# A graph attention kernel: queues of the opening stage, a staging pool of its own, and 17 of 18 edge tiles in two parts

## The chip, the cores and the metric

The kernel runs as one program on one core of a Trainium2 chip. The metric is the device time of one execution in microseconds (us). Engines are called TensorE (PE, with its weight loads shown as PEld), VectorE (DVE), ScalarE (ACT), GpSimd (POOL) and SyncE (SP), as in the profile. A queue is called by the engine that issues its transfers.

## The reference

Two graph attention layers stand between a normalization and residual paths. There are 3125 nodes with 768 features and 53125 edges, self loops among them, sorted by destination. All data is float32.

```python
def gat_conv(x, edge_index, W, a_src, a_dst, bias, heads, out_ch, concat):
    xl = (x @ W).reshape(n, heads, out_ch)
    alpha_src = jnp.einsum('nhc,hc->nh', xl, a_src)
    alpha_dst = jnp.einsum('nhc,hc->nh', xl, a_dst)
    e = jax.nn.leaky_relu(alpha_src[src] + alpha_dst[dst], 0.2)
    m = jax.ops.segment_max(e, dst, num_segments=n)
    e = jnp.exp(e - m[dst])
    s = jax.ops.segment_sum(e, dst, num_segments=n)
    alpha = e / (s[dst] + 1e-16)
    out = jax.ops.segment_sum(xl[src] * alpha[:, :, None], dst, num_segments=n)
    ...
h0 = jnp.maximum(_layernorm(x), 0.0)
h = gat_conv(h0, edge_index, W1, a_src1, a_dst1, b1, 4, 256, True)
h1 = relu(layer_norm(h, g1, be1)) + (h0 @ Wr1 + br1)
h = gat_conv(h1, edge_index, W2, a_src2, a_dst2, b2, 1, 768, False)
x + layer_norm(h, g2, be2) + (h1 @ Wr2 + br2)
```

Layer 1 has four heads of 256 channels, so W1 and Wr1 are 768 x 1024; W2 and Wr2 are 1024 x 768.

## The kernel before

**Tiling.** The nodes lie in NB = 25 blocks of P = 125. Edges of one block fill J = 18 tiles of 128 edges. Feature dimensions are cut into chunks of 128: NK1 = 6 for 768 and NK2 = 8 for 1024. Four blocks make a group of GB = 4, for which the residual product h0 @ Wr1 is made at once.

**The opening stage (0 to 209 us).** One loop, `for b in range(-2, NB + LAG)`, holds several streams. `fetch` loads a tile of x into one of eight buffers; tiles up to 4 are loaded by SP, later ones by POOL. `stats` (L600 to L604) and `normal` (L611, L612) make the layer norm on VectorE, with the square root `bn_sd` on ScalarE. `flip` transposes a block on TensorE (L623) and ScalarE writes it to `h0` (L625). `fill` is the generator `products` (L637 to L654): it multiplies a block by W1 (L645), ScalarE copies the two halves of 512 columns into `row` (L648, two buffers), and `store_rows` sends the finished row block to `table1` with two transfers on SP (L651). `work` is the generator `beside`: it counts edges by block (`edge_list`, L220, with a matmul over the counts at L228), has SP load the 25 edge windows of two kinds (`windows`, 50 loads), and folds the attention vectors into W1 on VectorE (`fold`, L308 and L309), which `alphas` (L633) needs. W1 is loaded by six transfers on ScalarE's queue (L691). The order of the instructions on ScalarE, VectorE and TensorE is the one written in the program, and an engine that waits holds what stands behind it.

**Softmax of layer 1 (209 to 481 us).** VectorE and TensorE compute the attention weights of all edges (L375 to L480); what remains of `products` is filled in on TensorE, and its last rows are drained after that.

**Between softmax and layer 1 (481 to 548 us).** VectorE folds the attention vectors of layer 2 into W2 (L730, L731), chunk by chunk, with tiles from a pool "wf". TensorE makes the residual product of group 0 (L739, 8 pieces of six matmuls, each recorded twice), ScalarE copies a piece to `rt0` (`copy_residual`, L577), and SP stores pairs of pieces into `r1T_d` (L581). The pool "rf" of `rt0` is opened after "wf" has been closed, so both lie on the same memory.

**Layer 1 (548 to 1547 us).** `sums` runs over the blocks. For each edge tile POOL gathers 128 rows of `table1` (L525, ten buffers), and VectorE makes a matrix `oh` (L536) that says which node of the block each edge ends at. A tile for which `split(j)` is true is multiplied by its attention weights in two parts: ScalarE makes a rounded product `hi` (four L543, one for each head) and VectorE the remainder in the place of `g` (four L544), and TensorE takes four matmuls of 512 columns in a faster float format (L548). A tile that isn't split has the weights multiplied into `oh` by ScalarE (four L558), and TensorE takes plain float32 matmuls of 256 columns, one for each head (L560). In between run the residual products of groups 1 to 6 (`residual`, L769) until about the 20th block, and behind each block its end, `end1`: layer norm, transposes (L801), relu (L803), residual added (L805), the product with W2 (L814). A block's last edge matmul is the one with the bias, L564.

```python
sums(H, C1, table1, al1, alo1_d, b1_r, lambda j: j % 9 != 4, 10, 4, 0, gp, pp, end1, later())
```

With `j % 9 != 4`, tiles 4 and 13 of 18 aren't split.

**Layer 2 (1547 to 2471 us)** repeats softmax and sums with one head of 768 channels.

Of the kernel before, what the change touches and what calls it, by code (L numbers as in the profile page):

```python
# [58 lines left out]
def in_order(  # L59
# [16 lines left out]
    nc = tc.nc  # L76
# [59 lines left out]
    def load_rows(q, t, src_, b):  # L136


        if b < NB - 1:
            q.dma_start(t, src_[b * P:b * P + 128, :])  # L140
        else:
            q.dma_start(t[:112], src_[b * P:b * P + 112, :])
            q.dma_start(t[112:P], src_[b * P + 112:(b + 1) * P, :])

    def store_rows(q, dst_, b, t):
        q.dma_start(dst_[b * P:b * P + 112, :], t[:112])
        q.dma_start(dst_[b * P + 112:(b + 1) * P, :], t[112:P])
# [424 lines left out]
    with tc.tile_pool(name="m1", bufs=1) as mp:  # L572
# [10 lines left out]
        with tc.tile_pool(name="w1", bufs=1) as wp, tc.tile_pool(name="pm1", bufs=1, space=PSUM) as pm1:  # L583
# [3 lines left out]
            with tc.tile_pool(name="d1", bufs=2) as dp, tc.tile_pool(name="pd1", bufs=1, space=PSUM) as pp:  # L587
                xts = {}

                def fetch(b):  # L590
                    xts[b] = dp.tile([128, D], F32, name="xt", bufs=AHEAD)
                    load_rows(nc.sync if b < 5 else nc.gpsimd, xts[b], x, b)

                found = {}

                def stats(b):
                    xt = xts[b][:P]
                    st = dp.tile([P, 2, 6], F32, name="bn_st", bufs=4)
                    for i in range(2):
                        nc.vector.bn_stats(st[:, i, :], xt[:, i * (D // 2):(i + 1) * (D // 2)])  # L600
                    mv = dp.tile([P, 2], F32, name="bn_mv", bufs=4)
                    nc.vector.bn_aggr(mv, st)
                    sd = dp.tile([P, 1], F32, name="bn_sd", bufs=4)
                    nc.scalar.activation(sd, mv[:, 1:2], AF.Sqrt, bias=eps[:P])  # L604
                    found[b] = mv, sd

                def normal(b):
                    xt = xts[b][:P]
                    mv, sd = found.pop(b)
                    rstd = dp.tile([P, 1], F32, name="bn_rs", bufs=4)  # L610
                    nc.vector.reciprocal(rstd, sd)  # L611
                    nc.vector.tensor_scalar(xt, xt, mv[:, 0:1], rstd, op0=OP.subtract, op1=OP.mult)  # L612

                def flip(b):

                    gi, o = b // GB, (b % GB) * P
                    if o == 0:
                        h0.append(wp.tile([128, NK1, min(GB, NB - b) * P], F32, name=f"h0_{gi}"))
                    xt = xts.pop(b)[:P]
                    for k0 in range(0, NK1, 3):  # L620
                        pt = pp.tile([128, 4, 128], F32, name="pt", bufs=3)
                        for k in range(3):
                            nc.tensor.transpose(pt[:, k, :P], xt[:, (k0 + k) * 128:(k0 + k + 1) * 128],  # L623
                                                ident[:P, :P])
                        nc.scalar.activation(h0[gi][:, k0:k0 + 3, o:o + P], pt[:, :3, :P], AF.Relu)  # L625
                    if b + AHEAD < NB:
                        fetch(b + AHEAD)

                def alphas(b):
                    gi, o = b // GB, (b % GB) * P  # L630
                    pa = pp.tile([P, 2 * H], F32, name="pas", bufs=1)
                    for k in range(NK1):
                        nc.tensor.matmul(pa, h0[gi][:, k, o:o + P], wa1[:, k, :],  # L633
                                         start=(k == 0), stop=(k == NK1 - 1))
                    return lambda: nc.vector.tensor_copy(asad1[:, b, :], pa)

                def products():  # L637

                    for b in range(NB):
                        gi, o = b // GB, (b % GB) * P  # L640
                        row = wp.tile([P, HC], F32, name="row", bufs=2)
                        for i in range(2):
                            pm = pm1.tile([128, 512], F32, name="pm", bufs=3)
                            for k in range(NK1):
                                nc.tensor.matmul(pm[:P], h0[gi][:, k, o:o + P], w1[:, k, i * 512:(i + 1) * 512],  # L645
                                                 start=(k == 0), stop=(k == NK1 - 1))
                                if k == NK1 - 1:
                                    nc.scalar.activation(row[:, i * 512:(i + 1) * 512], pm[:P], AF.Copy)  # L648
                                if k % 3 == 2:
                                    if i == 1 and k == NK1 - 1:  # L650
                                        store_rows(nc.sync, table1, b, row)  # L651
                                        if gi and (b % GB == GB - 1 or b == NB - 1):
                                            nc.sync.dma_start(h0T_d[gi][:, :, :o + P], h0[gi])
                                    yield  # L654

                fill = products()
                AHEAD, LAG = 8, 10

                def beside():

                    with tc.tile_pool(name="el", bufs=1) as ep:
                        listed = edge_list(ep, pp)
                        next(listed)
                        yield
                        for _ in listed:
                            yield
                    lists = windows(pp)
                    next(lists)
                    yield from fold(abs1, w1, NK1, H, C1, wa1)
                    for _ in lists:  # L670
                        yield

                work = beside()
                order = ctx.enter_context(ExitStack())
                order.enter_context(tc.manual_schedule(engines={PE}))
                with tc.manual_schedule(engines={ACT, DVE}):
                    fetch(0)
                    fetch(1)
                    next(work)
                    for b in range(2, 4):  # L680
                        fetch(b)
                    abs1 = folded(mp, H, C1, a_src1, a_dst1, "wr1", 2)
                    for b in range(4, AHEAD):
                        fetch(b)
                    late = None
                    for b in range(-2, NB + LAG):
                        if b + 2 < NB:
                            stats(b + 2)
                        if b == -1:
                            for k in range(NK1):  # L690
                                nc.scalar.dma_start(w1[:, k, :], W1[k * 128:(k + 1) * 128, :])  # L691
                        if 0 <= b + 1 < NB:
                            normal(b + 1)
                        if 0 <= b < NB:
                            flip(b)
                        if b >= 0:
                            next(work, None)
                        if late is not None:
                            late()
                            late = None  # L700
                        for _ in range(0 if b < 2 else 2 if b < LAG else 1 if b < NB or b % 2 else 0):
                            next(fill)
                        if b >= LAG:
                            late = alphas(b - LAG)
                    late()
                    for _ in work:
                        pass
                    for _ in range(3):
                        next(fill)
            with tc.tile_pool(name="pq1", bufs=1, space=PSUM) as pp:  # L710
# [6 lines left out]
                split_biases(mp)  # L717
                for _ in fill:
                    pass

                with tc.tile_pool(name="wf", bufs=2) as fp:
                    ab2 = fp.tile([128, 2, C2], F32, name="ab2", bufs=1)
# [7 lines left out]
                            nc.vector.tensor_tensor(t, w2k, ab2[:, i, :], OP.mult)  # L730
                            nc.vector.tensor_reduce(wa2[:, k, i:i + 1], t, axis=AX.X, op=OP.add)  # L731

                rp = order.enter_context(tc.tile_pool(name="rf", bufs=1))
                for m in range(NK2):
                    if m % 2 == 0:
                        rt = rp.tile([128, GB, 2, P], F32, name="rt0", bufs=4)
                    pm = pm1.tile([128, 512], F32, name="pm", bufs=3)
                    for k in range(NK1):
                        nc.tensor.matmul(pm[:, :GB * P], wr1[:, k, m * 128:(m + 1) * 128], h0[0][:, k, :],  # L739
                                         start=(k == 0), stop=(k == NK1 - 1))  # L740
                    copy_residual(0, rt, pm, m, GB)
# [3 lines left out]
        with tc.tile_pool(name="w2", bufs=1, reuse_waits="tile") as wp, tc.tile_pool(name="e1", bufs=2, reuse_waits="tile") as ep, \  # L745
# [74 lines left out]
                        nc.vector.tensor_copy(asad2[:, b, :], pm[:, 384:n])  # L820
                store_rows(nc.sync, table2, b, row)

            sums(H, C1, table1, al1, alo1_d, b1_r, lambda j: j % 9 != 4, 10, 4, 0, gp, pp, end1, later())


    with tc.tile_pool(name="m2", bufs=1, reuse_waits="tile") as mp, \
# [556 lines left out]
```

## Time and profile before

| what | value |
|---|---|
| time, median of three runs | 2466.43 us |
| time, lowest and highest of the three | 2462.73 and 2474.13 us |
| the profiled execution's own time | 2472.55 us |
| its span (first to last instruction) | 2470.7 us |
| granted TensorE clock, mean of the span | 0.952 |
| busy PE / DVE / ACT / POOL | 2255.8 / 1941.0 / 1276.1 / 1138.2 us |
| bytes moved by DMA | 637.97 MB, mean 258 GB/s |
| opening stage, to the loop's end | 0 to 209 us |
| softmax of layer 1 and drained rows | 209 to 481 us |
| group 0's residual beside the fold of W2 | 481 to 548 us |
| layer 1 | 548 to 1547 us |
| layer 2 | 1547 to 2470.7 us |

The profiled execution is 6.1 us above the median of the three. A line of a group in the profile gives code line, engine, operation, the tiles (out<-in), the shapes and the count, then the busy time in us and the mean ns of one. A line of the waits gives the engine and code line that waited, the work that released it, and the sum, the number and the longest of the waits in us. A line of the windows gives a stretch, its length, and for each engine the busy time and the number of instructions, then the granted clock of TensorE, the busy share of the DMA engines and the GB/s moved. A busy TensorE isn't TensorE at its peak, and a matmul of plain float32 is recorded as two.

### The profile page before, as it was taken

What the parts mean: (1) busy time and instruction counts of PE and PEld (TensorE: products, weight loads), DVE (VectorE), ACT (ScalarE), POOL (GpSimd) and SP (SyncE); (2) the same over time, 40 slices, a digit from 0 to 9 for tenths busy, and PEclk for the clock granted to TensorE, in tenths of its full rate; (3) what the DMA queues carried; (4) which work ended last, traced back from release to release, by engine and by line L of the source; (5) the groups of instructions that cost most, each with busy time, mean ns of one, the idle gap of its engine ahead of it and who ended that gap; (6) DMA issues with size and microseconds to landing.
All of it is one profiled execution on the core that took longest, in us unless ns stands there. A gap on an engine that the chain in (4) does not pass through costs nothing.

```text
span 2470.7 us, 35867 instructions
## 1 busy us (share of the span) xinstructions
PE 2255.8 (91%) x11254; PEld 1477.1 (60%) x11254; DVE 1941.0 (79%) x4328; ACT 1276.1 (52%) x2687; POOL 1138.2 (46%) x980
## 2 busy tenths in 40 slices
PE   3898999959899999999999999799798998989987
PEld 2465665425566666666666776566476665656655
DVE  5845999647788888888889999587677776768777
ACT  1221332117788888888888898001244444444443
POOL 0000000006756565555555675000477777777775
PEclk9898999978999999999999999899899899999999
DMA  5453552429788888888988898784698898888886
GB/s 169 134 178 115 192 182 70 146 86 397 260 301 311 297 317 296 298 315 289 324 285 304 317 340 277 286 297 158 203 309 304 301 311 295 291 290 295 290 287 210
DMA packets 185508, 637.97 MB, mean 258 GB/s; under 512 B 31924, under 2 KB 49189, under 8 KB 184542
## 3 DMA queue, kind: packets, MB, share of 16 engines
q0 software_dynamic: 104032, 420.88, 49.9%
q1 hardware_dynamic: 76564, 201.94, 23.6%
q10 hardware_dynamic: 4714, 12.75, 1.5%
q8 instruction: 94, 1.54, 0.2%
q14 instruction: 104, 0.85, 0.1%
HBM read 567.40 MB, written 68.08 MB: 257 GB/s over the span
## 4 chain that ended last, share of the span: by engine, by line
PE 69%; DVE 17%; DMA 6%; issue 5%; SPq 1%; ACT 1%; POOL 0%; ACTq 0%; DVEq 0%; POOLq 0%
PE pa L548 22%; PE p L814 10%; PE pa L560 9%; PE pr L769 8%; PE pr L848 8%; PE pm L645 5%; DVE g L544 2%; DVE scr L394 2%; DVE al L397 2%; PE pq L392 1%; PE pas L633 1%; PE pm L739 1%; PE pa L564 1%; DMA g<-table,idx_s 1%; DMA bs<-slo_d 1%
## 5 line engine op out<-in xcount | busy, mean ns | idle before, releaser
L525 POOL DMA_INDIRECT g<-table,idx_s x900 | 1064.4, 1183 | 958.7 <-DMA ab<-in_L_gnn_a_dst_dram 349.4
L543 ACT ACTIVATE hi<-g,al 128x256 fp32r<-128x256 f32 (+1 forms) x1925 | 966.6, 578 | 495.2 <-DMA g<-table,idx_s 177.8
L544 DVE SCALAR_TENSOR_TENSOR g<-g,al,hi 128x256 fp32r<-128x256 f32 (+1 forms) x1925 | 993.2, 566 | 78.7 <-issue 44.5
L548 PE MATMUL pa<-hi,oh 128*125 128x512 f32 (+1 forms) x1450 | 585.9, 482 | 41.6 <-issue 27.3
L548 PE MATMUL pa<-g,oh 128*125 128x512 f32 (+1 forms) x1450 | 448.4, 385 | 35.7 <-issue 30.5
L548 PEld LDWEIGHTS pa<-hi,oh 128*125 128x125 f32 x1450 | 268.1, 189 | 228.8 <-issue 119.0
L548 PEld LDWEIGHTS pa<-g,oh 128*125 128x125 f32 x1450 | 268.1, 189 | 97.1 <-issue 45.0
L848 PE MATMUL pr<-wr,h 128*125 128x384 f32 x800 | 308.6, 518 | 4.1 <-issue 2.7
L536 DVE TENSOR_SCALAR oh<-iota_f,rel_s 128x128 fp32r<-128x128 f32 x775 | 211.5, 283 | 127.2 <-PE pa L548 92.8
L560 PE MATMUL pa<-g,w 128*125 128x384 f32 (+1 forms) x900 | 291.7, 455 | 10.0 <-issue 8.4
L814 PE MATMUL p<-w,h1T 128*125 128x384 f32 (+1 forms) x800 | 298.5, 492 | 1.5 <-DVE h1T L805 1.5
L645 PE MATMUL pm<-w,h 128*125 128x512 f32 x600 | 285.2, 625 | 0.0
L769 PE MATMUL pr<-h0k,wr 128*128 128x500 f32 (+1 forms) x576 | 260.5, 538 | 1.9 <-DMA h0k<-h0T_d 1.9
L560 PEld LDWEIGHTS pa<-g,w 128*125 128x125 f32 x900 | 170.9, 194 | 96.9 <-issue 46.0
L848 PEld LDWEIGHTS pr<-wr,h 128*125 128x125 f32 x800 | 155.0, 199 | 92.1 <-issue 23.5
L814 PEld LDWEIGHTS p<-w,h1T 128*125 128x125 f32 x800 | 148.0, 188 | 78.5 <-issue 10.1
L645 PEld LDWEIGHTS pm<-w,h 128*125 128x125 f32 x600 | 113.7, 197 | 126.8 <-issue 126.7
L769 PEld LDWEIGHTS pr<-h0k,wr 128*128 128x128 f32 x576 | 106.4, 191 | 46.8 <-DMA h0k<-h0T_d 5.3
L392 PEld LDWEIGHTS <-ohs 125*128 125x128 bf16 x2700 | 101.7, 98 | 52.0 <-DVE ohs L380 34.6
L512 DVE SCALAR_TENSOR_TENSOR z<-own,aw,pa 125x256 f32<-125x256 f32 (+1 forms) x150 | 69.8, 521 | 77.7 <-PE pa L548 42.2
L392 PE MATMUL pq<-tabs,ohs 125*128 125x100 bf16 (+1 forms) x2700 | 105.6, 192 | 25.5 <-DVE ohs L380 21.9
L648 ACT ACTIVATE row<-pm 125x512 f32<-125x512 f32 x50 | 29.8, 595 | 170.3 <-PE pm L645 137.7
(194 smaller groups left out, 1636.8 us busy)
## 6 DMA issues: line engine op xcount, KB each, us to landing
bd<-dst_d SPq DMA_DIRECT2D x50, 576.0 KB
bs<-slo_d SPq DMA_DIRECT2D x50, 576.0 KB
g<-table,idx_s POOLq DMA_INDIRECT x900
r1T_d<-rt SPq DMA_DIRECT2D x100, 125.0 KB
r1t<-r1T_d SPq DMA_DIRECT2D x25, 500.0 KB
h1T_d<-h1T SPq DMA_DIRECT2D x25, 500.0 KB
h<-h1T_d SPq DMA_DIRECT2D x25, 500.0 KB
own<-table SPq DMA_DIRECT2D x24, 512.0 KB
```

What stands on the lines that cost most here:

```text
L392: nc.tensor.matmul(q[:, j], ohs[:P, (j0 + j) * 128:(j0 + j + 1) * 128], tabs[:, i], start=(i == 0), stop=(i == 2))
L512: nc.vector.scalar_tensor_tensor(z[:, o:o + n], own[:P, o:o + n], aw[:, o // cols:o // cols + 1], pa[:, o // f, o % f:o % f + n], op0=OP.m ...
L525: nc.gpsimd.indirect_dma_start(out=gf, out_offset=None, in_=table[:, :], in_offset=bass.IndirectOffsetOnAxis(ap=idx_s[:, c:c + 1], axis=0))
L536: nc.vector.tensor_scalar(oh, iota_f, rel_s[:, c:c + 1], None, op0=OP.is_equal)
L543: nc.scalar.activation(hi[:, cs], gf[:, cs], AF.Copy, scale=a)
L544: nc.vector.scalar_tensor_tensor(g[:, cs], gf[:, cs], a, hi[:, cs].bitcast(F32), op0=OP.mult, op1=OP.subtract)
L548: nc.tensor.matmul(pa[:, i, :f], oh[:, :P], t[:, i * f:(i + 1) * f], start=(j == 0 and t is hi), stop=False)
L560: nc.tensor.matmul(pa[:, o // f, o % f:o % f + n], w[:, o // cols, :], gf[:, o:o + n], start=(j == 0), stop=False)
L645: nc.tensor.matmul(pm[:P], h0[gi][:, k, o:o + P], w1[:, k, i * 512:(i + 1) * 512], start=(k == 0), stop=(k == NK1 - 1))
L769: nc.tensor.matmul(pm[:, :nb * P], wr1[:, k, m * 128:(m + 1) * 128], loaded[gi, k][:, :nb * P], start=(k == 0), stop=(k == NK1 - 1))
L814: nc.tensor.matmul(pm[:, :n], hT[:, k, :], w2[:, k, o:o + n], start=(k == 0), stop=(k == NK2 - 1))
L848: nc.tensor.matmul(pm[:, :384], h1[:, k, :], wr2[:, k, i * 384:(i + 1) * 384], start=(k == 0), stop=False)
```

## The change

It has three parts.

1. In the opening stage, x tile 4 and the row stores of `table1` go from SP's queue to POOL's. W1 goes from six transfers on ScalarE's queue to twelve half ones on POOL's, the first column half of all chunks, then x tiles 4 and 5, then the second half, then tiles 6 and 7; a VectorE `memset` of a few elements of W1, placed after the statistics of the second tile, stands ahead of these loads. The two attention vectors for the fold of W1 (`abs1`) are loaded later, in iteration b = 1. In each iteration the `fill` steps come ahead of the `work` step.
2. The pool "rf" of the residual staging of group 0 is opened ahead of "wf", on the other side of the memory, with three `rt0` buffers for four.
3. In layer 1, tile 8 alone isn't split: 17 of 18 tiles are split, where 16 were.

```diff
-                    load_rows(nc.sync if b < 5 else nc.gpsimd, xts[b], x, b)
+                    load_rows(nc.sync if b < 4 else nc.gpsimd, xts[b], x, b)
...
-                                        store_rows(nc.sync, table1, b, row)
+                                        store_rows(nc.gpsimd, table1, b, row)
...
-                    abs1 = folded(mp, H, C1, a_src1, a_dst1, "wr1", 2)
-                    for b in range(4, AHEAD):
-                        fetch(b)
                     late = None
                     for b in range(-2, NB + LAG):
                         if b + 2 < NB:
                             stats(b + 2)
                         if b == -1:
-                            for k in range(NK1):
-                                nc.scalar.dma_start(w1[:, k, :], W1[k * 128:(k + 1) * 128, :])
+
+                            nc.vector.memset(w1[:, :, 0:HC:512], 0.0)
+                            for i in range(2):
+                                for k in range(NK1):
+                                    nc.gpsimd.dma_start(w1[:, k, i * 512:(i + 1) * 512],
+                                                        W1[k * 128:(k + 1) * 128, i * 512:(i + 1) * 512])
+                                fetch(4 + 2 * i)
+                                fetch(5 + 2 * i)
+                        if b == 1:
+                            abs1 = folded(mp, H, C1, a_src1, a_dst1, "wr1", 2)
                         if 0 <= b + 1 < NB:
                             normal(b + 1)
                         if 0 <= b < NB:
                             flip(b)
+                        for _ in range(0 if b < 2 else 2 if b < LAG else 1 if b < NB or b % 2 else 0):
+                            next(fill)
                         if b >= 0:
                             next(work, None)
                         if late is not None:
                             late()
                             late = None
-                        for _ in range(0 if b < 2 else 2 if b < LAG else 1 if b < NB or b % 2 else 0):
-                            next(fill)
...
+                rp = order.enter_context(tc.tile_pool(name="rf", bufs=1, side="right"))
                 with tc.tile_pool(name="wf", bufs=2) as fp:
...
-                rp = order.enter_context(tc.tile_pool(name="rf", bufs=1))
...
-                        rt = rp.tile([128, GB, 2, P], F32, name="rt0", bufs=4)
+                        rt = rp.tile([128, GB, 2, P], F32, name="rt0", bufs=3)
...
-            sums(H, C1, table1, al1, alo1_d, b1_r, lambda j: j % 9 != 4, 10, 4, 0, gp, pp, end1, later())
+            sums(H, C1, table1, al1, alo1_d, b1_r, lambda j: j % 18 != 8, 10, 4, 0, gp, pp, end1, later())
```

## The prediction

> **What bounds the kernel now.** I read the page's totals and chain first, then windows by stage, then waits and timeline of the three places that the change touches.
>
> ```profile
> PE 2255.8 (91%) x11254; PEld 1477.1 (60%) x11254; DVE 1941.0 (79%) x4328; ACT 1276.1 (52%) x2687; POOL 1138.2 (46%) x980
> PE 69%; DVE 17%; DMA 6%; issue 5%; SPq 1%; ACT 1%; POOL 0%; ACTq 0%; DVEq 0%; POOLq 0%
> ```
>
> TensorE carries 69% of the chain, VectorE 17%. The windows (stretch, length, then busy us of PE, PEld, DVE, ACT, POOL, then TensorE's granted clock, DMA share, GB/s) show where PE is free:
>
> ```profile
> 99.50:117.00 17.50, 16.80 (x68) 10.24 (x69) 11.47 (x20) 3.73 (x11) 1.08 (x2) 0.63 0.68 252
> 209.00:430.00 221.00, 205.23 (x2118) 129.99 (x2118) 210.18 (x281) 66.45 (x74) 0.00 (x0) 0.97 0.44 143
> 496.50:519.50 23.00, 0.00 (x0) 0.00 (x0) 22.38 (x27) 0.71 (x2) 0.00 (x0) 0.61 0.29 85
> 519.50:548.00 28.50, 28.26 (x60) 12.40 (x60) 0.00 (x0) 4.00 (x7) 0.00 (x0) 0.90 0.17 54
> 548.00:598.50 50.50, 37.59 (x104) 21.46 (x104) 33.65 (x94) 32.65 (x80) 28.61 (x28) 0.76 0.98 376
> 689.00:1376.80 687.80, 687.80 (x2484) 449.12 (x2483) 595.40 (x1632) 570.55 (x1446) 396.92 (x323) 1.00 0.88 303
> 1376.80:1546.70 169.90, 166.67 (x707) 120.99 (x706) 164.31 (x456) 156.35 (x407) 113.71 (x82) 0.99 0.88 313
> ```
>
> Layer 1's softmax (209 to 430) is VectorE's. From 496.5 to 519.5 PE does nothing while VectorE folds W2. Blocks 3 to 19 of layer 1 (689 to 1376.8) are PE without a gap, VectorE 87% busy; in the last five blocks, where the residual products have run out, both are full. The waits (engine, line, released by: us in total, times, longest), first two lines up to 110 us, the rest from 480 to 560:
>
> ```profile
> ACT bn_sd L604 <- DMA w<-in_L_gnn_W_dram: 19.3, 1, 19.3
> ACT row L648 <- DMA table<-row: 13.9, 1, 13.9
> ...
> POOL g L525 <- DMA g_c<-in_L_gnn_g_dram: 64.6, 1, 64.6
> ACT rt L577 <- DVE wa2s L731: 36.9, 1, 36.9
> DVE oh L536 <- DMA r1T_d<-rt: 33.0, 1, 33.0
> PE pm L739 <- ACT rt L577: 23.2, 1, 23.2
> ```
>
> **Part 1, the front: −19.** Before, ScalarE's queue issues the six W1 loads from 6.18 to 25.8, so a `bn_sd` that normalization needs stands 19.3 behind them; the counts' matmul (L228) comes at 48.64 and the fifth block's transposes at 56.75. Then the row store is issued by SP, which stands behind 50 window loads until 95; that is the 13.9 wait of `row`, and PE idles 7.6 before 99.56. The first alpha products (L633) start at 105.36; from there PE is full to 208.8, the loop's end. So the gain here is how much earlier L633 starts. After: W1 is issued by POOL behind x tiles 0 to 3, and ScalarE issues nothing. I walk the changed order with these durations. VectorE waited 10.8 for x tile 2, which landed at 18.3 among W1's 3.1 MB; first in line it lands near 9.5 (four tiles, 1.5 MB, at the 330 GB/s of the first 25 us). Block 2's transposes come near 15, the first product near 17 (half of W1, 1.6 MB, 5 us behind). The counts are 25 × 0.67 (L220 and its accumulator read) with normalization between; without the 10.8 and with some 4 of a 7.0 wait for bias vectors gone, their matmul comes near 34, block 4 near 35, 20 earlier. That some of this walk is off by an iteration (5.8) is in the bounds. Next VectorE is the bound: folding W1 costs a multiply and a reduce of 1.22 each, twice per chunk, with normalization 6.7 an iteration; before it ran 63.9 to 104.8, after it starts some 20 earlier. L633 near 85±4: gain 15 to 24, I take 19. A new PE idle of 8 to 11 before L633 stays inside this, as does the half-clock stretch.
>
> What moves: 12 half loads of W1, one x tile and 50 row-store DMAs go onto POOL's queue. POOL's x load takes 573 ns each (L140 x19), so 63 × 0.57 = 36 us of POOL, which up to 481 has 13 us of work; no row wait is expected, since a row buffer is used again only two rows later (two rows 38 us apart or more in the softmax, 20 in the drain after it) against 3.3 for a store (issued at 95.07, its waiter free at 98.36). Queued behind a store on POOL: x loads, eight tiles ahead. The added memset (128x12) is under 0.2 of VectorE. SP loses 51 DMAs; window loads no longer delay stores. The alpha `ab` loads move later but were needed only at the fold.
>
> Here a rule speaks against the change. The row: 573 ns of POOL per x load. The Trainium skill, "DMA: Bandwidth & Descriptors", section "Issuing engine by pattern", gives simple loads and stores to Sync and calls that path generally faster; its section "SWDGE vs HWDGE vs iDMA" adds that GpSimd writes descriptors into SBUF state from which VectorE can lock it out in a 2-port mode. By the rule I would charge the latency difference that page states (about 1 against 0.6 us) on all 63, 25 us, and the front would gain nothing net; by the rows nothing of it lies on the path. I take the rows, and keep +25 as the upper end for POOL issue. The lock-out shows nowhere before, because POOL has no work from 209 to 481; gathers in layer 1 ran 1.23 us mean beside a VectorE 87% busy, the nearest row.
>
> **Part 2, residual staging: −30.** Before, rt0 lies where "wf" was, so the first copy (L577) waits 36.9 for the fold's last L731, and PE, out of PSUM, 23.2. With a pool of its own on the right side, the copy waits only for the softmax's last VectorE work (477) and its matmuls. Three buffers for four: the fourth pair waits for stores of the first, long done. So 96 L739 matmuls run from 481.05 without the 23.0 gap, and without the slow clock behind it: 60 records took 28.3, against 60 × 0.424 = 25.4 (pace of the warm ones), 2.9 more. L739 ends near 521.8, not 547.8: −26. VectorE's fold ends at 517.5 either way, beside it.
>
> A rule again: "TensorE: Matmul & The Clock Gate", Part 1, says the clock halves after one idle window and returns after about 3.4 us of sustained work; that would give 3.4 × half = 1.7 here; the trace has 2.9, and 0.63 over 17.5 us in the first window above. I use the trace.
>
> Then the start of layer 1. Its second gather waited to 553.08 (64.6), `oh` to 551.95, both for rt0's memory. After, neither waits for rt0; the gathers wait for the fold's last read, near 518. The stage to 598.5 is DMA-bound (share 0.98, 376 GB/s), so freeing gathers 30 earlier moves 9 MB of gathers plus w2 and the next residual's operands 30 earlier, not faster; b1_r, w2 and h0k loads sit on SP behind the residual stores, and these come 25 earlier. Block 0 ends near 565 to 570, not 598.5: bounds −24 (transfers collide with the residual stores) and −35; I take −30, which holds the −26 and the moved tile of block 0.
>
> **Part 3, 17 of 18 tiles split: −8.** A split tile is four L548 (start, us, engine, line, operation):
>
> ```profile
> 1024.04 0.62 PE L548 MATMUL pa<-g,oh 128*125 128x512 f32 x2
> 1024.50 0.63 PE L548 MATMUL pa<-hi,oh 128*125 128x512 f32 x2
> 1024.97 0.64 PE L548 MATMUL pa<-g,oh 128*125 128x512 f32 x2
> ...
> 1039.96 1.89 PE L560 MATMUL pa<-g,w 128*125 128x256 f32 x8
> 1041.69 1.14 PE L814 MATMUL p<-w,h1T 128*125 128x384 f32 x3
> ```
>
> Pairs start 0.465 apart: 0.93 a tile. Unsplit, all of its L560: 1041.69 − 1039.96 = 1.73. So −0.80 per block for the one moved tile. VectorE gets four L544 more at 0.415 (451.1 busy us in that window over 1088), +1.66; ScalarE four L543 (457.0 over 1089, 0.42) in place of four shorter L558, at most +0.4. Blocks of 40.46 have VectorE 35.0, so 36.7 under 39.66: PE still binds, 19 blocks × −0.80 = −15. The last five blocks have VectorE at 164.3 of 169.9, idle 1.1 a block; I let 0.2 of that be usable, since its waits are short ones between tiles: 5 × (1.66 − 0.2) = +7. Net −8; ends −16 (tail hidden) and +8 (VectorE binds half of the blocks).
>
> Sum −19 −30 −8 = −57. Layer 2 is untouched. Against the profiled run, 2472.55: 2415.5. That run is 6.1 above the median of the three (2466.43), so 2409.
>
> **Rivals.** *VectorE catches up* (0.25): the front yields only 10 because the fold finds VectorE full, and layer 1's blocks end 0 better with the tail's +7. −10 −28 +5 = −33, 2433. For it: VectorE 87% in blocks whose PE share I shorten, and the tail at 97%. Against: 3 us a block to spare.
>
> *Staging does not move the start* (0.10): DMA at 376 GB/s sets it, so only PE's gap goes. −19 −12 −8 = −39, 2427. For it: share 0.98. Against: from 496 to 548 the share was 0.17 to 0.29, room to start in.
>
> *POOL's stores are starved* (0.07), the other side: in the softmax, VectorE is 95% busy and locks POOL out, so a row store is issued late, `row` waits for its buffer, and PE, in order, holds the softmax's L392 behind the waiting fill product. It decides once a store lands later than two row cadences, about 38 us after its copy. From there each further us of each of some 15 rows is on the path; 6 us over gives +90, total +33, 2499. Against: nothing that VectorE runs there is longer than about 11 us.
>
> **How the numbers follow.** Main case 0.58, its own range 2398 to 2427 (the parts' ends, +4 −5, +6 −5 and +16 −8, combined as independent). The range 2392 to 2440 adds most of the two smaller gains and the case that layer 1 starts a little earlier still. Half a percent, about what can be told from no change, is 12.3 us: faster means under 2454. Main and the two smaller gains lie below it, less 0.05 for those gains shrinking further together: 0.88; same 0.05; slower 0.07.
>
> **What would show it.** Right: W1 off ACTq, no 19.3 wait; L633 first at 81 to 90; no PE gap between L739 records; second gather near 500 on the new axis; steady blocks 39.6 to 39.8; tail blocks about 1.4 longer. Wrong would be: `row` waiting for its store in the softmax; L739 held by ACT; steady blocks at 40.4 or more; softmax starting later than 195.

## The result

The changed kernel takes 2425.15 us (median of four runs, 2422.0 to 2429.11); the kernel before, with one more run, 2464.66 (2462.73 to 2474.13). The ratio is 0.9833, interval 0.9803 to 0.9863: 40 us faster. The profiled execution took 2423.72 with a span of 2421.8, 48.9 less than the span before. The totals of the page of the changed kernel:

```profile
PE 2236.3 (92%) x11154; PEld 1456.2 (60%) x11154; DVE 1972.1 (81%) x4429; ACT 1289.0 (53%) x2687; POOL 1205.3 (50%) x1043
```

100 matmul records fewer and 101 VectorE instructions more are the 25 tiles that are split now; the 63 more on POOL are the transfers. (Behind the edit, line numbers are larger by up to 5: L739 is now L744, L769 L774, L814 L819.) For the sum, instants are better than averages. They are from the timelines of the two profiled executions, in us:

| instant | before | changed | shift | gained or lost in this stage |
|---|---|---|---|---|
| the first block's twelve L633 done | 106.78 | 94.96 | −11.8 | |
| the loop's last L633 starts | 208.63 | 202.23 | −6.4 | |
| softmax's last VectorE work (L480) starts | 473.72 | 466.42 | −7.3 | front −7.3 |
| first L739 (L744) | 481.05 | 473.7 | −7.3 | 0 |
| its last one done | 547.8 | 514.2 | −33.6 | −26.3 |
| block 0 of layer 1 ends (L564) | 598.52 | 569.43 | −29.1 | +4.5 |
| block 2 ends | 689.08 | 653.32 | −35.8 | −6.7 |
| block 19 ends | 1376.79 | 1333.26 | −43.5 | −7.8 |
| block 24 ends | 1546.73 | 1511.36 | −35.4 | +8.2 |
| end of span | 2470.7 | 2421.8 | −48.9 | −13.5 |

The last row is layer 2, which the change doesn't touch: it took 924.0 in that trace of before and 909.6 to 919.8 in five other traces with the same granted clock there (0.93), so most of the 13.5 is its own variation, and −35 to −40 is what the change did. The windows of the changed kernel, in the columns of those before:

```profile
473.70:514.20 40.50, 40.45 (x97) 18.05 (x95) 29.48 (x41) 5.37 (x9) 7.08 (x8) 1.00 0.62 188
514.20:569.40 55.20, 35.82 (x100) 20.76 (x100) 33.52 (x91) 33.94 (x85) 24.68 (x20) 0.78 0.85 309
653.32:1333.26 679.94, 675.48 (x2415) 435.36 (x2415) 617.52 (x1700) 580.61 (x1446) 427.92 (x323) 1.00 0.89 307
1333.26:1511.36 178.10, 169.30 (x687) 114.72 (x686) 172.19 (x477) 161.00 (x411) 116.61 (x82) 1.00 0.85 299
```

PE works through the residual of group 0 at full clock (first line). Then comes a stretch with PE busy 36 of 55 us. In the 17 steady blocks (3 to 19) PE isn't full any more, 4.5 us idle, and the tail (last line) is VectorE's, 172 of 178. The waits show the new places; the first two lines are from the first 110 us, the rest from 455 to 560:

```profile
ACT bn_sd L604 <- DVE ball_hi L165: 17.5, 1, 17.5
DVE b_hi L165 <- DMA b_v<-in_L_gnn_b_dram: 11.3, 1, 11.3
...
POOL g L525 <- DMA r1T_d<-rt: 24.4, 1, 24.4
PE pr L774 <- DMA h0k<-h0T_d: 15.3, 1, 15.3
```

W1's 19.3 on ScalarE is gone, and another of 17.5 stands in its place, behind VectorE's wait for bias vectors, which grew from 7.0 to 11.3. In the kernel before that line is:

```profile
DVE b_hi L165 <- DMA b_v<-in_L_gnn_b_dram: 7.0, 1, 7.0
```

The splitting of the biases stands behind the loop in the program; it was scheduled into the loop, so there the order isn't the written one. The 23.2 of PE behind the residual copies is gone, and PE waits 15.3 for `h0k`, the operand of the next residual. The 24.4 of the second gather is put down to a store of `rt`, but it ends 0.3 us after the fold's last multiply (L736, to 508.28), and in e4_h0k_first and e10_best below the same wait is put down to the fold, so the fold is the likelier cause, as forecast.

### The profile page after: what moved, and what is told of

Same layout as the page of the kernel before. It is cut to its first block, busy times and chain, and to the rows that moved or that the text cites. A ratio compares the mean times of both kernels' runs of the same rounds, so it can differ in the third digit from the quotient of the medians.

```text
span 2421.8 us, 35879 instructions
## 1 busy us (share of the span) xinstructions
PE 2236.3 (92%) x11154; PEld 1456.2 (60%) x11154; DVE 1972.1 (81%) x4429; ACT 1289.0 (53%) x2687; POOL 1205.3 (50%) x1043
## 5 line engine op out<-in xcount | busy, mean ns | idle before, releaser
L525 POOL DMA_INDIRECT g<-table,idx_s x900 | 1102.8, 1225 | 530.4 <-PE pa L548 273.6
L543 ACT ACTIVATE hi<-g,al 128x256 fp32r<-128x256 f32 (+1 forms) x2025 | 1002.0, 574 | 442.1 <-DMA g<-table,idx_s 160.8
L544 DVE SCALAR_TENSOR_TENSOR g<-g,al,hi 128x256 fp32r<-128x256 f32 (+1 forms) x2025 | 1032.2, 560 | 58.7 <-issue 40.7
L548 PE MATMUL pa<-hi,oh 128*125 128x512 f32 (+1 forms) x1500 | 611.2, 486 | 32.4 <-issue 24.2
L548 PE MATMUL pa<-g,oh 128*125 128x512 f32 (+1 forms) x1500 | 469.2, 387 | 28.8 <-issue 20.1
L548 PEld LDWEIGHTS pa<-hi,oh 128*125 128x125 f32 x1500 | 279.0, 190 | 229.4 <-issue 107.6
L548 PEld LDWEIGHTS pa<-g,oh 128*125 128x125 f32 x1500 | 278.4, 189 | 96.6 <-DVE g L544 29.0
L853 PE MATMUL pr<-wr,h 128*125 128x384 f32 x800 | 307.1, 514 | 10.7 <-issue 7.4
L819 PE MATMUL p<-w,h1T 128*125 128x384 f32 (+1 forms) x800 | 298.1, 492 | 1.8 <-DVE h1T L810 1.5
L645 PE MATMUL pm<-w,h 128*125 128x512 f32 x600 | 286.9, 629 | 0.0
L774 PE MATMUL pr<-h0k,wr 128*128 128x500 f32 (+1 forms) x576 | 258.5, 537 | 15.5 <-DMA h0k<-h0T_d 15.3
L560 PE MATMUL pa<-g,w 128*125 128x384 f32 (+1 forms) x700 | 241.5, 472 | 12.4 <-ACT w L558 7.0
L819 PEld LDWEIGHTS p<-w,h1T 128*125 128x125 f32 x800 | 147.9, 188 | 81.4 <-issue 10.0
L645 PEld LDWEIGHTS pm<-w,h 128*125 128x125 f32 x600 | 114.9, 199 | 127.8 <-issue 127.1
L146 POOL DMA_DIRECT2D table<-row x25 | 14.3, 572 | 352.1 <-ACT row L648 325.1
L560 PEld LDWEIGHTS pa<-g,w 128*125 128x125 f32 x700 | 130.6, 191 | 81.9 <-issue 19.2
L774 PEld LDWEIGHTS pr<-h0k,wr 128*128 128x128 f32 x576 | 105.2, 192 | 58.9 <-DMA h0k<-h0T_d 16.6
```

What stands on the lines that cost most here:

```text
L525: nc.gpsimd.indirect_dma_start(out=gf, out_offset=None, in_=table[:, :], in_offset=bass.IndirectOffsetOnAxis(ap=idx_s[:, c:c + 1], axis=0))
L543: nc.scalar.activation(hi[:, cs], gf[:, cs], AF.Copy, scale=a)
L544: nc.vector.scalar_tensor_tensor(g[:, cs], gf[:, cs], a, hi[:, cs].bitcast(F32), op0=OP.mult, op1=OP.subtract)
L548: nc.tensor.matmul(pa[:, i, :f], oh[:, :P], t[:, i * f:(i + 1) * f], start=(j == 0 and t is hi), stop=False)
L560: nc.tensor.matmul(pa[:, o // f, o % f:o % f + n], w[:, o // cols, :], gf[:, o:o + n], start=(j == 0), stop=False)
L774: nc.tensor.matmul(pm[:, :nb * P], wr1[:, k, m * 128:(m + 1) * 128], loaded[gi, k][:, :nb * P], start=(k == 0), stop=(k == NK1 - 1))
```

## The experiments

The runs e1 to e4 shared a chip with a median of 2460.49 for the kernel before, e5 to e8 a second one, where it takes 2427.24, and e9 to e12 a third, where it takes 2422.07 (layer 2 is faster on both). So times are compared between chips as ratios and stage lengths only. "Stage" is the time from the start of L480, the softmax's last VectorE work, to the end of block 24 in the trace: 1073.0 before, 1044.9 changed.

### The parts, each alone

**Part 1 alone** (e1_front): the diff shown above without the pool, the `rt0` and the `split` lines.

> Part 1 alone on the kernel before (queues of x, W1 and rows, fill ahead of work); staging and tiles as before. Theory A: the bias loads behind W1 hold VectorE to 32, so the front gives only what the changed kernel's trace shows at the softmax's last VectorE instruction (466.4 for 473.7): about -7 us, and nothing of it is lost or won later, 2457. Rival, the working of the prediction: -19, and something in the other parts gave it back, 2446. Rival of starved stores: over 2465, with a row copy waiting for its store.

Measured: 2447.74, ratio 0.9956 (0.9941 to 0.9972), −11. L480 at 462.40, stage 1071.8: all of the gain lies ahead of the softmax's end, and no row copy waited for a store. With 11.3 it fell between the two theories, nearer the lower one. On this chip traces without part 1 (e2, e3) have L480 at 476.3 and 472.4, and traces with it (e1, e4) at 462.4 and 465.4; with the 473.7 and 466.4 of the table, the front's gain is 6 to 14, about 9, not a fixed number.

**Part 2 alone** (e2_staging).

```diff
+                rp = order.enter_context(tc.tile_pool(name="rf", bufs=1, side="right"))
                 with tc.tile_pool(name="wf", bufs=2) as fp:
...
-                rp = order.enter_context(tc.tile_pool(name="rf", bufs=1))
...
-                        rt = rp.tile([128, GB, 2, P], F32, name="rt0", bufs=4)
+                        rt = rp.tile([128, GB, 2, P], F32, name="rt0", bufs=3)
```

> Part 2 alone on the kernel before (pool rf opened ahead of wf, on the right side, three buffers). Theory A: L739 runs through, its end 26 earlier, but the first residual operand h0k stands behind W2's eight loads and gives 4 back: block 0 ends 22 earlier, near 577, the time near 2443. Prediction's working: -30, 2435. Rival that the DMA sets the start of layer 1: -12, 2453.

Measured: 2429.74, ratio 0.989 (0.9864 to 0.9916), −27; stage 1040.9, −32. Block 0 ends at 581.13 with L480 at 476.28 (2.6 later than before, by chance of the front): 20 less, near the 22 expected, and PE waited 15.9 for `h0k` here too. But 10 more came in block 2, which neither theory had. Before, that block had a hole, with PE idle for 6.6 us:

```profile
638.74:689.08 50.34, 43.75 (x148) 27.92 (x147) 35.04 (x98) 33.79 (x86) 33.74 (x25) 0.90 0.80 279
```

and with the staging alone it is a steady block:

```profile
620.25:660.68 40.43, 40.43 (x148) 26.41 (x147) 35.01 (x97) 33.58 (x86) 24.35 (x19) 1.00 0.86 299
```

The hole's first sign in the trace of before is VectorE idle for 10.7 us ahead of `iso` (start, us, instruction, idle before):

```profile
648.38 0.16 DVE L507 TENSOR_TENSOR iso<-ao,node_f 125x1 f32<-125x1 f32 x1 [10.68 <-issue]
```

The profile names no releaser. `iso` reads `ao`, a gather by POOL; POOL issued three of them only from 640.92 to 645.6, behind gathers of 4.8, 2.9 and 5.9 us. Why this comes late isn't settled. Where it stands in the program doesn't decide it alone: in the six traces with all three parts and `h0k` behind W2 (changed, e5, e6, e8, e9, e12) the longest wait ahead of an `iso` at this point is the same instruction's, 0.7, 0.8, 6.8, 1.1, 2.6 and 2.6 us, and block 2 takes 40.6, 40.9, 46.2, 39.9, 42.3 and 42.1.

**Part 3 alone** (e3_split).

```diff
-lambda j: j % 9 != 4
+lambda j: j % 18 != 8
```

> Part 3 alone on the kernel before (17 of 18 tiles split). Theory A: 0.75 less in each of 19 blocks, 14 in all, and 8 more in the last five: -6, near 2459. Rival, VectorE binds the blocks: no change in the steady blocks and +8 in the tail, 2473.

Measured: 2452.87, ratio 0.9963 (0.9946 to 0.998), −8 to −9. The total agrees with both the −6 and the prediction's −8, and the trace says why neither reason holds in full: blocks 3 to 19 cost 680.2 for 687.7 (−7.5, half of the 14), the tail 180.2 for 169.9 (+10.3), and block 2 lost its hole (40.95 for 50.34, −9.4). Without the hole's 9.4 the part alone would be near zero.

So the parts alone, 11 + 27 + 8, sum to 46, and together they give 40: the hole goes with part 2 as with part 3, and is counted twice.

**Parts 1 and 2 without 3** (e7_all16): the changed kernel with `j % 9 != 4`.

> The changed kernel without its third part: 16 of 18 tiles split in all blocks. Theory A: the 17 blocks from 653 to 1333 cost 7.8 more, the tail 8.2 less, so the third part is worth nothing beside the other two: within 3 us of 2425; no wait of 10 us in block 2, since staging has removed it too. Rival, the prediction's working (-8 for this part): 2433. Rival, that part 3 removed the 10 us in block 2: 2435.

Measured: ratio 0.9808 (0.9774 to 0.9842), with no hole in block 2 (40.43). The ratio's interval overlaps that of the changed kernel (0.9803 to 0.9863), so the times decide nothing. The stage is shorter: 1038.7, against 1042.6 to 1047.3 in five traces with all three parts. By it, part 3 costs 4 to 9 us beside part 2, and 6 against the trace of the changed kernel: without it +7.8 in the steady blocks, −9.7 in the tail, −4.3 in blocks 1 and 2. Its windows, steady and tail:

```profile
645.03:1332.75 687.72, 687.72 (x2484) 449.15 (x2483) 595.39 (x1632) 570.30 (x1446) 397.02 (x323) 1.00 0.88 303
1332.75:1501.13 168.38, 165.64 (x707) 119.68 (x707) 164.01 (x456) 157.22 (x407) 117.24 (x82) 1.00 0.88 316
```

### The missing 20 us at the start of layer 1 and in the tail

**h0k ahead of W2** (e4_h0k_first).

```diff
             be1_c = by_chunk(be1, wp, NK2, "be1_c")
-            for k in range(NK2):
-                nc.sync.dma_start(w2[:, k, :C2], W2[k * 128:(k + 1) * 128, :])
...
             for k in range(NK1):
                 load(1, k)
+            for k in range(NK2):
+                nc.sync.dma_start(w2[:, k, :C2], W2[k * 128:(k + 1) * 128, :])
```

> The changed kernel, with the six h0k loads issued ahead of the eight loads of W2 at the start of layer 1; nothing else edited. Theory A: the wait of 15.3 us of PE at L774 (530.5 to 545.9) came from SP's order, so it goes or falls under 5 us, block 0 ends near 558 in place of 569.4, and the time is 8 to 12 us under the changed kernel's, near 2415. Rival: the DMA engines are full from 514 to 554 whatever the order, so another transfer (gathers, then W2 for L819) is late in its place; block 1 or 2 gives the time back, within 3 us of 2425.

Measured: 2408.48, ratio 0.979 (0.9771 to 0.9809). Block 0 ends at 559.26 (569.43 in the changed kernel), and the 10 stay to the end of layer 1: stage 1033.1, −11.8. SP's issues tell it (start, us, queue, line), first the changed kernel, then this one:

```profile
521.71 13.35 SPq L757 DMA_DIRECT2D w<-in_L_gnn_W_dram  x8
536.67 6.87 SPq L764 DMA_DIRECT2D h0k<-h0T_d  x6
```

```profile
521.03 8.12 SPq L762 DMA_DIRECT2D h0k<-h0T_d  x6
529.19 4.64 SPq L789 DMA_DIRECT2D w<-in_L_gnn_W_dram  x8
```

With the DMA engines full (share 1.05), the eight issues took SP 13.35 us, the first of them 6.83, and `h0k` was first issued at 536.7. Issued first, it lets PE go on at 529.7 and not 545.9. A wait of 11.8 stays, so the "under 5" of the expectation was wrong; W2, later now, is in time: no L819 waits for it. The rival, that another transfer late in its place gives the time back, is refuted.

**16 of 18 in the tail** (e6_tail16): `split(j)` becomes `split(j, b)`, with

```diff
-lambda j: j % 18 != 8
+lambda j, b: j % 18 != 8 if b < 20 else j % 9 != 4
```

> The changed kernel, with 17 of 18 tiles split in blocks 0 to 19 and 16 of 18 in the last five. Theory A: VectorE binds the last five blocks; they take 170 again in place of 178.1, time near 2417. Rival: the tail is long for another reason (gathers, order), and stays at 176 or more.

Measured: ratio 0.9765 (0.973 to 0.9801), stage 1038.6; the last five blocks take 170.2, as expected, and the stage is 6 shorter than that of the changed kernel. That PE waits for VectorE in the 17-of-18 tail is in the waits of PE there, the changed kernel first, 16 of 18 (e7_all16) after it:

```profile
PE pa L548 <- DVE g L544: 6.0, 16, 1.0
```

```profile
PE pa L548 <- DVE g L544: 1.7, 3, 1.2
```

### The missing 12 us of the front

**Biases split later** (e5_bias_late).

```diff
                     for b in range(-2, NB + LAG):
+                        if b == 16:
+                            split_biases(mp)
...
-                split_biases(mp)
```

> The changed kernel, with the splitting of the biases put into VectorE's written order in iteration b = 16 in place of where the scheduler had put it (behind the ninth count). Theory A: the 11.3 us that VectorE waited for the bias loads is what kept the counts at 45.7 where the prediction had 34; so L228 comes near 35, the first full L633 near 86 in place of 94.8, and the softmax's last VectorE instruction 7 to 9 earlier than 466.4; time near 2417. Rival: what follows (the fold on VectorE, or the slow clock from 165 to 205) takes the gain back: L228 earlier, the softmax's end within 2 us, time 2425.

Measured: ratio 0.9778 (0.9744 to 0.9811). L228 comes at 33.99, which is the prediction's 34; the last two of the first L633 come at 82.64 and not 94.38, and L480 starts at 456.6, where the three other traces of that chip have 460.4 to 462.6. So 11.7 at the fold, and 4 to 6 at the softmax's end. Both theories are half right. The windows from the first block's last L633 to the last transposes, the same 357 matmul records, show where the other half goes, without this edit (e7_all16, same chip) and with it:

```profile
94.62:159.73 65.11, 64.50 (x357) 43.76 (x358) 37.93 (x96) 18.58 (x46) 7.86 (x13) 0.97 0.44 159
```

```profile
82.64:154.05 71.41, 69.74 (x357) 46.99 (x358) 38.89 (x103) 18.60 (x46) 8.16 (x13) 0.90 0.41 146
```

The granted clock is 0.90 for 0.97. With the edit PE waits 1.7 us for a VectorE copy (`asad`, L635) at 117, and from 118.1 to 124.9 the granted clock is 0.5; e10_best below has the same wait and 0.5 from 118.0 to 121.4. That the wait brings the clock down isn't shown. What follows the last transposes, L645 and L633 alone, is slow in every trace: 35.8 to 40.4 us at a clock of 0.89 to 0.79, with no clear order between that and when it begins (152 to 173).

**Which edit of part 1 gained** (e11_fill_order), on the kernel before: the two lines of `fill` moved above `next(work, None)`, queues as before.

> The kernel before with one edit of part 1: in each iteration the fill steps come ahead of the work step; queues as before. Theory A: the front's gain comes from the order, since PE does a product where it waited 9.75 us for the counts: L633 6 to 10 earlier, ratio 0.996 to 0.997. Rival, it comes from W1 leaving ScalarE's queue: L633 within 2 us, ratio 0.999 to 1.001.

Measured: ratio 0.995 (0.9932 to 0.9968), −12. Two moved lines give as much time as all of part 1 (0.9956). PE now makes a product where it had waited for the counts, the kernel before first, this one after it:

```profile
38.08 0.81 PE L623 MATMUL pt<-ident,xt 125*128 125x125 f32 x6
48.64 0.25 PE L228 MATMUL pe<-cnt,ones 125*1 125x26 f32 x2 [9.75 <-DVE ones L226]
```

```profile
39.49 0.81 PE L623 MATMUL pt<-ident,xt 125*128 125x125 f32 x6
40.13 5.32 PE L645 MATMUL pm<-w,h 128*125 128x512 f32 x12
49.13 0.21 PE L228 MATMUL pe<-cnt,ones 125*1 125x26 f32 x2 [3.68 <-DVE ones L226]
```

The first block's last two L633 come at 97.78, where all twelve came at 105.36. W1's queue by itself is next.

**W1 back on ScalarE** (e12_w1_act), in the changed kernel.

```diff
-                            for i in range(2):
-                                for k in range(NK1):
-                                    nc.gpsimd.dma_start(w1[:, k, i * 512:(i + 1) * 512],
-                                                        W1[k * 128:(k + 1) * 128, i * 512:(i + 1) * 512])
-                                fetch(4 + 2 * i)
-                                fetch(5 + 2 * i)
+                            for k in range(NK1):
+                                nc.scalar.dma_start(w1[:, k, :], W1[k * 128:(k + 1) * 128, :])
+                            for i in range(4, AHEAD):
+                                fetch(i)
```

> The changed kernel with W1 loaded by six transfers on ScalarE's queue as in the kernel before; everything else as changed. Theory A, the order is what gained: within 3 us of the changed kernel. Rival, W1 on ScalarE holds bn_sd and the transposes again: L228 at 48 or later, 4 to 10 us slower than the changed kernel.

Measured: ratio 0.9844 (0.9814 to 0.9873), the same as the changed kernel beside it (0.9845). The `bn_sd` wait is back with 19.0 and L228 at 48.62, as the rival says, yet the first block's last two L633 are only 3 later (97.31), and the medians differ by 2.2 us. The single traces leave more open: L480 is at 466.5 here and at 466.3 in e11_fill_order, and at 459.6 in the unedited e9_again on the same chip, where traces of one front differed by up to 4 on the first chip. So a cost of a few us isn't excluded, but most of the 19.0 of wait cost nothing.

**Row stores back on SP** (e8_rows_sp).

```diff
-                                        store_rows(nc.gpsimd, table1, b, row)
+                                        store_rows(nc.sync, table1, b, row)
```

> The changed kernel with the row stores of table1 back on SP. Theory A: a store on SP stands behind the 50 window loads once more, so a row copy on ScalarE waits 10 or more us near 80 to 95, and L633 comes later: the softmax's end 2 to 6 later than 466.4, time 2427 to 2431. Rival, the rule that stores from POOL are the slower ones: 3 to 10 us faster than 2425, the softmax shorter.

Measured: ratio 0.9831 (0.9793 to 0.9869), L480 at 460.39 (462.4 and 462.6 with the rows on POOL on that chip), stage 1044.2. Neither theory: no row copy waits for its store even on SP, since with `fill` ahead of `work` the scheduler puts the first row's store among the window loads, at 61.15, and the next at 92.94 in time. The queue of the row stores makes no difference that these runs can tell.

### The changed kernel again, and a version that beats it

**The changed kernel again** (e9_again), unedited, on the chip of the best version.

> The changed kernel unedited, beside the runs of this call, so that they can be set against it on the same chip. Both theories: ratio to the kernel before 0.983, the stage from the softmax's last VectorE instruction to the end of the last block of layer 1 at 1044 to 1046 us.

Measured: 2383.15, ratio 0.9845 (0.981 to 0.988), stage 1047.3, a little over the 1044 to 1046 expected.

**Three edits together** (e10_best): those of e4_h0k_first, e5_bias_late and e6_tail16.

> The changed kernel with three edits: h0k loads ahead of W2's, biases split in iteration 16, and 16 of 18 tiles split in the last five blocks. Theory A: they lie in different stages, so they add: 6 from the biases (after the slow clock has taken half of 12), 12 from h0k, 6 to 8 from the tail, 24 to 26 under the changed kernel, ratio to before 0.972 to 0.974. Rival: they overlap as parts 2 and 3 did; ratio 0.977 or more.

Measured: 2350.5, ratio 0.9705 (0.9672 to 0.9738), 33 under the changed kernel on the same chip, its interval below the other's. L480 455.84, stage 1014.3 for 1047.3. The gain is larger than the sum of 24 to 26: in the traces 3.8 comes ahead of L480, 10.0 to the end of block 0 and 10.8 in the tail, where 6, 12 and 6 to 8 were expected of the three edits, and besides 6.5 in blocks 1 and 2 and 5.8 in the steady blocks, which became full again:

```profile
626.78:1301.77 674.99, 674.55 (x2415) 435.68 (x2414) 617.73 (x1702) 581.60 (x1450) 441.39 (x324) 1.00 0.90 309
1301.77:1470.12 168.35, 166.50 (x708) 121.05 (x707) 163.98 (x456) 157.17 (x407) 116.03 (x82) 0.99 0.88 316
```

PE is idle 0.4 us in those 17 blocks, against 5.0 in the changed kernel beside it. Why the short waits are gone (PE waited seven times, 5.0 us in all, for a ScalarE `w` in e9_again) is not settled; other versions with 17 of 18 in these blocks have 676.7 to 680.2. Whether 16 of 18 in all blocks would do as well beside the other two edits wasn't run.

## Why the prediction was right, and where it wasn't

The direction and the main mechanism were right, and 2425 lies in the range, but 16 us above 2409. Of the 57 forecast, 35 were found up to the end of layer 1. Of its signs, PE has no gap between the L739 records and no row copy waits for its store, as forecast; the second gather comes at 508.6 for 500, a steady block takes 40.0, between the 39.8 of right and the 40.4 of wrong, and a tail block is 1.6 longer for 1.4. Term by term:

- **Front, −19: was −7 in this trace (6 to 14 on one chip).** The first steps of the walk held: the third block's transposes came at 15.96 for 15, the first product at 17.24 for 17. The step that failed let "some 4 of a 7.0 wait for bias vectors" go. The wait grew to 11.3. VectorE reached `b_hi` early, at 20.5, but the loads, issued on SP from 17.2 among the transfers of W1 and x, let it go on only at 31.8. So the counts came at 45.73 for the predicted 34, and the last two of the first L633 at 94.38, not 85; the first eight, at 86.21, lie inside the 81 to 90 that was to show the walk right, and say nothing of it. With the biases out of the way the walk's 34 was met (33.99, and 33.75 in e10_best). A second step was missed: the loop after L633 isn't a fixed 103 us. From the first block's last L633 to the loop's last one, nearly the same matmuls took 100.9 to 110.2 us in the fourteen traces, at a mean granted clock of 0.94 to 0.87; it was 103.6 in the trace of before and 108.1 in that of the changed kernel. And the credit went to the wrong edit: the order of `fill` and `work`, which the prediction didn't cost, gives the time of all of part 1, and moving W1 or the rows back loses no time that the runs can tell.
- **PE gap of the staging, −26: was −26.3.** 23.0 of wait and 2.9 of slow clock, as read from the trace.
- **Start of layer 1, −30 with the gap: was −22.** The prediction named the queue ("h0k loads sit on SP behind the residual stores") and then moved them 25 earlier as a block. It put no time on the issue of W2's eight loads ahead of `h0k`, which took 13.35 us with the DMA engines full, so PE waited 15.3. The rival "staging does not move the start" had the cause, but priced it too high (PE's gap only, −12).
- **Block 2, 0: was −10** (−6.7 with block 1, which took 3 longer). Not seen: the hole was in the trace of before, and taken as something that stays.
- **Part 3, −8: is +4 to +9 beside part 2, by the traces.** Steady, −15 was forecast for 19 blocks and −7.8 measured for 17, in which PE's busy time fell by 12.2, near the forecast (0.72 a block for 0.80), and 4.5 of new idle time, 4.3 of it for ScalarE's `w`, ate a third. The tail's +7 was +8.2. The step that failed is "PE still binds" from two averages, 36.7 under 39.7: blocks with VectorE at 91% and PE at 99% still have five waits of PE for ScalarE in those 17.
- **POOL's row stores.** The rule that charged them with 25 us was rightly set aside: no row copy waits for a store from 205 to 430, while VectorE was busy 210 of 225; on SP they cost the same. The lock-out of which the Trainium skill, "DMA: Bandwidth & Descriptors", section "SWDGE vs HWDGE vs iDMA", warns doesn't show there: POOL's 22 row stores in that stretch took 0.51 to 0.99 us each.
- **Luck.** 2425 is nearest to 2427, the number of the rival "staging does not move the start", whose terms −19, −12 and −8 were −7, −22 and about 0 (steady −7.8, tail +8.2). The 6.7 of blocks 1 and 2, which no case held, brought the result nearer to 2409 too.

## What to carry to other kernels

Removing the wait that ends last buys the distance to the next one: walk the queue of the transfer that is needed next in issue order, with issue times as they are when the DMA engines are full, and put what is consumed first at the head of it. Parts that fill the same hole don't add, so measure each with the others in place: part 3 alone was 8 faster, and beside part 2 it cost some 6 by the trace. Before moving transfers between queues, try the order of work on the engine that idles; two moved lines gave as much time as all of part 1.

## What the runs showed of the hardware that I had not expected

- With the DMA engines at a share of 1.04 to 1.08, the first of the loads that SP issued behind the small vectors at the start of layer 1 took 4.4 to 10.0 us to issue in the ten traces with part 2, whether it was W2's or `h0k`'s, and the queue held everything behind it; in the four without, at 0.88 to 0.96, it took 0.6 to 0.7. A single load at other times takes 0.32.
- TensorE's granted clock was 0.77 to 0.85 from 160 to 205 us in the eleven traces with `fill` ahead of `work`, in the changed kernel with PE busy 43.6 of 45 us and idle steps of at most 0.35, in a phase of twelve 8-column matmuls (L633) around six 512-column ones. The Trainium skill, "TensorE: Matmul & The Clock Gate", Part 1, ties the drop to an idle window of about 3.4 us, or to frequent micro-idles between groups of matmuls; no such window is in the trace there, and whether the short steps are the cause no run here shows.
- The unchanged layer 2 took 909.6 to 924.0 us in the traces with a clock of 0.93 in it, and 868.5 to 880.8 on the two other chips, at 0.96 to 0.97.
